# One transformer layer on one core: softmax reciprocals moved from GpSimd to VectorE, routing ahead of other deferred work, and a new order of the last rows

## The chip, the cores and the metric

The kernel runs on one core of one Trainium2 chip. The core has a matrix engine (TensorE, PE in the profile), VectorE (DVE), ScalarE (ACT), GpSimd (POOL) and queues that start DMA transfers; SyncE's queue is SP. Each engine runs its own instructions in order and waits on semaphores for the others. The metric is the device time in microseconds (us) of one execution, as the median of several.

## The reference

The layer is `x = x + LN(attention(LN(x)))`, then `x = x + LN(ffn(LN(x)))`, in fp32, with 1024 rows of 512 elements. `LN` subtracts the mean and divides by the root of the variance plus 1e-5, without weights.

- Attention: `q = x @ w_q` gives 32 heads of 128, `k` and `v` 8 heads of 128, each shared by 4 query heads. Scores are scaled by 1/sqrt(128), masked causally, and go through a softmax; the weighted values of all heads are multiplied by `w_o` (4096 x 512).
- FFN: `base = x @ base_W.T + base_b`. A router gives 15 logits; their softmax is taken, the 8 largest are kept, and each is added to one of 8 experts by `expert_map`. The low-rank part is `h = x @ A.T` (8 experts of rank 16), scaled by the weight of its expert, times `B`, times 2, and is added to `base`.

## The kernel before

**Blocks.** The rows are cut into eight tiles of 128 (t = 0 to 7), and the heads into eight groups g of four query heads and one key head. A block is a pair (g, t); a row pair u is tiles 2u and 2u + 1. Groups 0 to 5 run over all tiles in turn; then groups 6 and 7 are taken together for the row pairs 0, 3, 2, 1, so the rows end in the order 0, 1, 6, 7, 4, 5, 2, 3 (`blocks`, lines 86 to 90). In the code c, d, e, f are the rows 4, 5, 2 and 3 that end last (line 657).

**One block.** `scores` (line 385) is called four times for a block, for sub-tiles j of 32 rows by 4 heads, which makes 128 partitions. For each: PE forms the scores `s` in PSUM, n columns of them up to the diagonal; DVE adds the mask to the last 32 columns (line 406) and takes the negated row maximum `nmax` (line 408); ACT takes the exponential into `p` with the row sum `total` (line 413); POOL takes `rec = total ** -1` (line 415). `finish`, run after the exponential of the next sub-tile has been put out, scales `p` by `rec` on ACT (line 420) and transposes it in 32 x 32 squares on DVE (line 424) into `T`. After the fourth sub-tile, `to_keys` (line 436) copies `T` into `K` with 16 DMAs, on SyncE's queue for nearly all blocks. Two blocks later `weighted_values` (line 446) multiplies `K` by `v` on PE (`po`), and ACT copies the result to `attnT`.

**Buffers.** Scores have two PSUM tiles of 1024 columns; in rows 0 to 3 two sub-tiles share one, so an odd one begins when the even one's exponential is through. All other products (`pq`, `pk`, `pv`, `pl`, `pf`, `ptx`, `ptw`, `pa` to `pe`, `pO`) share three PSUM banks (`bank`, line 239).

**Output projection.** For groups 0 to 6, `project_o_pair` (line 492) multiplies two row tiles at once by `w_o` in seven products `pa` to `pe`, with four sums of `attnT` blocks on DVE (`sums`, lines 501 to 504) and combined weights that POOL prepares (`combine_o`, line 478). The last group has the plain `project_o` (line 463, `pO`). When its sum is complete, `ffn_norms` (line 551) normalises the row, adds x and normalises again to `h`.

**FFN of a row.** `ffn_router` (line 569) transposes `h` on PE and copies it to `hT` with ACT, then multiplies it by the router and low-rank weights (`pl`). `route` (line 590) is a chain of nine small DVE steps from `recr` to `hw`. `ffn_out` (line 619) adds up `pf` from four base products, transposes `hw` (`ptw`) and adds the low-rank product; then y is normalised, on POOL for the rows that end early and on DVE for e and f, added to `acc`, and stored.

**Order.** PE's instructions, and all that pass through `keep` (line 92), stand in program order; other instructions are placed by a scheduler that estimates when each can run. `defer` (line 367) puts pieces of the FFN into a list; each call of `scores` works off one or more from its head (line 416). In the main loop (lines 773 to 802) each block's PE pieces (projections of q, k and v for later blocks, output projections, FFN products) are woven into one list, and a quarter of it by columns follows each sub-tile's scores (`run_share`, line 720). The tail (lines 805 to 820) has an order written out by hand. `prepare_ffn` (line 201) has six DMA issues on POOL and the casts of `emap_f`.

Of the kernel before, what the change touches and what calls it, by code (L numbers as in the profile page):

```python
# [22 lines left out]
def kernel(  # L23
# [145 lines left out]
    make_identity(nc, ident)  # L169
    neg_half = const.tile([P, 1], F32, tag="neg_half", name="neg_half")  # L170
    nc.gpsimd.memset(neg_half, -0.5)
    neg_one = const.tile([P, 1], F32, tag="neg_one", name="neg_one")
    nc.gpsimd.memset(neg_one, -1.0)

    xnT = [big.tile([P, KC, QB], F32, tag=f"xnT{b}", name=f"xnT_{b}") for b in range(NQB)]

# [41 lines left out]
    def layernorm(dst, src, name, by=nc.vector):  # L218

        got = []  # L220

        def statistics():
            stats = small.tile([P, 6], F32, tag="stats", name=f"stats_{name}")
            order(nc.vector.bn_stats(stats, src))
            mv = small.tile([P, 2], F32, tag="mv", name=f"mv_{name}")
            order(nc.vector.bn_aggr(mv, stats))
            ve = small.tile([P, 1], F32, tag="ve", name=f"ve_{name}")
            order(nc.vector.tensor_scalar(ve, mv[:, 1:2], EPS, None, ALU.add))
            rstd = small.tile([P, 1], F32, tag="rstd", name=f"rstd_{name}")
            order(nc.gpsimd.tensor_tensor(rstd, ve, neg_half, ALU.pow))  # L230
            got.extend((mv, rstd))

        def norm():
            mv, rstd = got
            order(by.tensor_scalar(dst, src, mv[:, 0:1], rstd, ALU.subtract, ALU.mult))

        return statistics, norm

    def bank(name):
        return ps_m.tile([P, 512], F32, tag="pm", name=name)  # L240

    def bank_pv(name):
        return ps_m.tile([P, 512], F32, tag="po", name=name, bufs=1)
# [120 lines left out]
    score_tile = {}  # L364
    deferred = []

    def defer(*steps):

        if score_tile:
            deferred.extend(steps)  # L370
        else:
            for step in steps:
                step()
# [5 lines left out]
    def finish_scores():  # L379


        if "finish" in score_tile:
            score_tile.pop("finish")()

    def scores(g, t, j):

        n = t * P + (j + 1) * SQ
        full = (t + 1) * P
        name = f"{g}_{t}_{j}"

        if t < TPB and j % 2:
            s = score_tile.pop(0)[:, QB:]
        else:
            s = ps_s.tile([P, S], F32, tag="s", name=f"s_{name}")
            score_tile[0] = s
        for c0 in range(0, n, QB):
            w = min(QB, n - c0)
            matmul(
                s[:, c0 : c0 + w],
                qTs[g, t // 2][:, (t % 2) * NSUB + j, :, :].rearrange("p h q -> p (h q)"),  # L400
                kTs[g, c0 // QB][:, :w],
                start=True,
                stop=True,
            )
        pin = keep if blocks.index((g, t)) >= N2 + 2 else lambda ins: ins
        pin(nc.vector.tensor_tensor(s[:, n - SQ : n], s[:, n - SQ : n], smask, ALU.add))  # L406
        nmax = small.tile([P, 1], F32, tag="nmax", name=f"nmax_{name}")
        pin(nc.vector.tensor_reduce(nmax, s[:, :n], AX.X, ALU.max, negate=True))  # L408
        p = act.tile([P, S], F32, tag="p", name=f"p_{name}", bufs=3)
        if n < full:  # L410
            nc.gpsimd.memset(p[:, n:full], 0.0)  # L411
        total = small.tile([P, 1], F32, tag="total", name=f"total_{name}")
        nc.scalar.activation(p[:, :n], s[:, :n], AF.Exp, bias=nmax, accum_out=total)  # L413
        rec = small.tile([P, 1], F32, tag="rec", name=f"rec_{name}")
        nc.gpsimd.tensor_tensor(rec, total, neg_one, ALU.pow)  # L415
        work_off(1 + len(deferred) // 5)
        finish_scores()

        def finish():
            keep(nc.scalar.mul(p[:, :n], p[:, :n], rec))  # L420
            if j == 0:
                turned[g, t] = turn_view(turn_tile("T", g, t), t)
            pin(
                nc.vector.transpose(  # L424
                    turned[g, t][:, :, j, :, :].rearrange("p b k q -> p k b q"),
                    p[:, :full].rearrange("p (k b q) -> p k b q", b=R, q=SQ),
                )
            )
            if j == NSUB - 1:
                three = (nc.sync, nc.sync, nc.gpsimd)  # L430
                alone = 3 <= blocks.index((g, t)) < N - 1
                to_keys(g, t, by=three[:1] if alone else three)

        score_tile["finish"] = finish

    def to_keys(g, t, by=(nc.sync,)):

# [131 lines left out]
    def ffn_router(t):  # L569
# [5 lines left out]

        def products():
            hT = state["hT", t]
            pl = bank(f"pl_{t}")[:, : NR + ER]
            for c in range(KC):
                matmul(pl, hT[:, c, :], ra_sb[:, c, :], start=(c == 0), stop=(c == KC - 1))  # L580
            lg = small.tile([P, NR], F32, tag="lg", name=f"lg_{t}")
            order(nc.vector.tensor_tensor(lg, pl[:, :NR], rb_bc, ALU.add))
            nmax = small.tile([P, 1], F32, tag="nmax", name=f"nmaxr_{t}")
            order(nc.vector.tensor_reduce(nmax, lg, AX.X, ALU.max, negate=True))
            ex = small.tile([P, NR], F32, tag="ex", name=f"ex_{t}")
            total = small.tile([P, 1], F32, tag="total", name=f"totalr_{t}")
            nc.scalar.activation(ex, lg, AF.Exp, bias=nmax, accum_out=total)
            defer(lambda: route(pl, ex, total))

        def route(pl, ex, total):  # L590
            rec = small.tile([P, 1], F32, tag="rec", name=f"recr_{t}")
# [27 lines left out]
    def ffn_out(t):  # L619

        pf = []

        def base(c):
            if c == 0:
                pf.append(bank(f"pf_{t}"))
            matmul(pf[0], state["hT", t][:, c, :], weights["base", c], start=(c == 0), stop=False)

        def turn_hw():
            pt = bank(f"ptw_{t}")
            transpose(pt[:, :ER], state.pop(("hw", t)).rearrange("p e r -> p (e r)"), ident)  # L630
            hwT = state["hwT", t] = ffn.tile([ER, P], F32, tag="hwT", name=f"hwT_{t}")
            nc.scalar.copy(hwT, pt[:, :P])

        def finish():
            matmul(pf[0], state.pop(("hwT", t)), bt_sb, start=False, stop=True)
            y = ffn.tile([P, H], F32, tag="hy", name=f"y_{t}", bufs=3)
            order(nc.vector.tensor_tensor(y, pf[0], bias_bc, ALU.add))
            by = nc.vector if t in (e, f) else nc.gpsimd
            statistics, norm = layernorm(y, y, f"y{t}", by)

            def add_y():
                norm()
                order(by.tensor_tensor(acc[t], y, acc[t], ALU.add))
                state["done", t] = True

            defer(statistics, add_y)

        w = [(512, lambda c=c: base(c)) for c in range(KC)]
        return w[:2], [(P, turn_hw)], w[2:], [(512, finish)]
# [10 lines left out]
    def projections(i):  # L660
# [22 lines left out]
        else:  # L683
            n = i - N2
            for k, what in ((0, (G - 1, 0)), (2, (G - 2, 1)), (3, (G - 1, 1))):
                if n == k:
                    other += project_k(*what)
            for t in {0: (0,), 1: (1,), 2: (2, 3), 3: (4, 5), 4: (6, 7)}.get(n, ()):
                other += project_v(g // GV, t)
        return q, other  # L690

    def loads(i):
# [6 lines left out]
        if i < N2:  # L699
            if t == 3:  # L700
                load_k(g + 1)
            if t == 5 and g + 1 == G - 2:
                load_k(G - 1)
            if t == 6 and (g + 1) % GV == 0:
                for j in range(2):
                    load_v((g + 1) // GV, j)
            if t == 5:
                load_o(g + 1)
        elif i == N2 + 3:
            load_o(G - 1)  # L710
        elif i == N2 + 4:
            load_base("wk", (0, 1))
        elif i == N2 + 5:
            load_base("wv", (2, 3))

    def run(pieces):
# [53 lines left out]
    def attend(i):  # L770
        return weighted_values(*blocks[i])

    for i in range(N):
        loads(i)
        for t in complete(i, 2):
# [10 lines left out]
        for t in complete(i, 5):  # L786
            begins = ffn_router(t)

        rest = o + weave(o_pair, begins[1:] + other + pv)
        then = begins[:1] + q + ends[:-1] + rest[:4] + ends[-1:] + rest[4:]  # L790
        for n in range(NSUB):
            scores(*blocks[i], n)
# [2 lines left out]
            combine_o(0)  # L795
        if i == NT:
            prepare_ffn()
        for t in complete(i, 7, 8):
            ffn_store(t)

        if i >= NT and blocks[i - 2][1] == 0 and blocks[i - 2][0] < G - 1:
            combine_o(blocks[i - 2][0])


    finish_scores()
    score_tile.clear()
    work_off(len(deferred))
# [2 lines left out]
    (turn_d, products_d), (turn_e, products_e), (turn_f, products_f) = map(ffn_router, (d, e, f))  # L810
    out_c, out_d, out_e, out_f = map(ffn_out, (c, d, e, f))
    o_pair = project_o_pair(*pairs[N // 2 - 2])
    run([turn_d] + weave(o_pair, [products_d] + attend(N - 2)))
    run(out_c[0] + out_c[1] + out_c[2] + attend(N - 1) + out_c[3])
    run(project_o(*blocks[N - 2]) + out_d[0] + project_o(*blocks[N - 1]))
    run(out_d[1] + out_d[2] + out_d[3])
    run([turn_e] + out_e[0][:1] + [products_e] + out_e[0][1:] + out_e[2])
    run([turn_f] + out_f[0] + [products_f] + out_e[1] + out_e[3] + out_f[2] + out_f[1] + out_f[3])
    for t in (c, d, e, f):
        ffn_store(t)  # L820


# [39 lines left out]
```

## Time and profile before

The median of 3 runs is 1117.16 us (1116.51 to 1117.96).

| What | Value |
|---|---|
| profiled execution, its own time | 1116.45 us |
| span from the first to the last instruction | 1114.7 us |
| mean granted PE clock | 0.992 |
| PE busy | 1077.6 us (97%) |
| DVE busy | 631.1 us (57%) |
| ACT busy | 464.5 us (42%) |
| POOL busy | 264.5 us (24%), of it 141.6 in 256 reciprocals (553 ns each) |
| PE waits for `hw` at `ptw` | 7.7 us in 3 waits |
| PE waits for exponentials at `s` | 7.5 us in 10 waits |

Busy time is given by engine; an idle engine costs time only where the work that ends last waits for it. A row of the page's list of groups has the source line, the engine, the operation, output and inputs with their shapes, the count, then the busy time in us and the mean duration in ns, and the idle time before. A row of the timeline has the start, the duration, then the same names, and in brackets how long the engine stood idle and for what. An fp32 product of 512 columns shows as two instructions, each about 0.43 us apart.

### The profile page before, as it was taken

To read this page: it belongs to the slowest core of one execution; us is meant where nothing else is said; L and a number is where in the kernel's file an instruction comes from. 1 tells how busy PE (TensorE), PEld (TensorE's weight loads), DVE (VectorE), ACT (ScalarE), POOL (GpSimd) and SP (SyncE) were. 2 spreads that over 40 slices of the span, in tenths; PEclk is the share of its full clock that TensorE was granted. 3 is DMA by queue.
4 is the path that set the end of the run, shared out by engine and by line. 5 is a ranking of instruction groups with operands and counts; after the bars stand their busy time and mean duration, and the time that the engine had idled before them with its cause. 6 is when DMAs were issued, how large, how long until landed. Compare 5 with 4: busy or idle time off the path is not lost.

```text
span 1114.7 us, 12767 instructions
## 1 busy us (share of the span) xinstructions
PE 1077.6 (97%) x3836; PEld 708.0 (64%) x3836; DVE 631.1 (57%) x1267; ACT 464.5 (42%) x985; POOL 264.5 (24%) x562
## 2 busy tenths in 40 slices
PE   8899999999999999999999999999999999989894
PEld 7576666667676666666676666666776556556442
DVE  4465545664465546665465545665336665665744
ACT  2554524444344434544344434543335443433400
POOL 2621123111321113111221123111131212323421
PEclk9999999999999999999999999999999999999997
DMA  5135352555135432455125432456234464451310
GB/s 179 39 104 139 70 116 57 142 129 112 34 90 132 90 86 58 120 138 122 35 70 149 95 85 56 124 135 164 61 124 114 114 158 97 111 155 41 94 46 28
DMA packets 79060, 111.82 MB, mean 100 GB/s; under 512 B 18176, under 2 KB 50560, under 8 KB 78992
## 3 DMA queue, kind: packets, MB, share of 16 engines
q1 hardware_dynamic: 52976, 82.08, 31.7%
q10 hardware_dynamic: 25040, 27.27, 7.7%
q0 software_dynamic: 976, 1.65, 0.6%
q8 instruction: 31, 0.51, 0.2%
q14 instruction: 37, 0.30, 0.1%
HBM read 33.34 MB, written 2.10 MB: 32 GB/s over the span
## 4 chain that ended last, share of the span: by engine, by line
PE 78%; DVE 7%; SPq 4%; ACT 4%; POOL 3%; DMA 2%; issue 2%; ACTq 0%; POOLq 0%
PE po L100 19%; PE s L100 17%; PE pq L100 16%; PE pv L100 5%; PE pk L100 4%; PE pa L100 4%; SPq L106 4%; PE pe L100 4%; PE pb L100 2%; DVE T L424 2%; PE pd L100 2%; ACT p L413 2%; PE pc L100 2%; PE pf L100 2%; ACT p L420 2%
## 5 line engine op out<-in xcount | busy, mean ns | idle before, releaser
L413 ACT ACTIVATE p<-s,nmax 128x32 f32<-128x32 f32 (+31 forms) x256 | 179.3, 700 | 416.4 <-DVE nmax L408 402.2
L424 DVE STREAM_TRANSPOSE T<-p 128x128 f32<-128x128 f32 (+7 forms) x256 | 198.8, 777 | 232.3 <-ACT p L420 209.5
L415 POOL TENSOR_TENSOR rec<-total,neg_one 128x1 f32<-128x1 f32 x256 | 141.6, 553 | 627.1 <-ACT p L413 623.3
L100 PE MATMUL s<-kT,qT 128*128 128x512 f32 (+15 forms) x768 | 273.7, 465 | 7.5 <-ACT p L413 7.5
L100 PE MATMUL po<-K,v 128*128 128x512 f32 x576 | 276.4, 594 | 1.3 <-DMA K<-T 0.7
L100 PE MATMUL pq<-xnT,wq 128*128 128x256 f32 x1024 | 235.8, 380 | 0.0
L100 PEld LDWEIGHTS s<-kT,qT 128*128 128x128 f32 x768 | 145.5, 191 | 133.3 <-issue 109.0
L100 PEld LDWEIGHTS pq<-xnT,wq 128*128 128x128 f32 x1024 | 193.3, 190 | 38.1 <-issue 15.5
L420 ACT ACTIVATE p<-p,rec 128x32 f32<-128x32 f32 (+31 forms) x256 | 185.3, 724 | 6.7 <-POOL rec L415 6.5
L408 DVE TENSOR_REDUCE nmax<-s 128x1 f32<-128x32 f32 (+31 forms) x256 | 180.9, 707 | 7.9
L100 PEld LDWEIGHTS po<-K,v 128*128 128x128 f32 x576 | 107.6, 190 | 75.8 <-issue 65.9
L406 DVE TENSOR_TENSOR s<-s,smask 128x32 f32<-128x32 f32 x256 | 48.9, 191 | 132.9 <-PE s L100 132.3
L100 PE MATMUL pv<-wv,xnT 128*128 128x256 f32 x256 | 68.0, 381 | 0.7 <-ACT xnT L250 0.7
L336 ACT ACTIVATE qT<-pq 128x512 f32<-128x512 f32 x64 | 38.0, 593 | 70.5 <-PE pq L100 70.5
L411 POOL MEMSET p<- 128x96 f32 (+2 forms) x192 | 28.8, 151 | 160.5 <-DVE T L424 156.1
L100 PE MATMUL pk<-xnT,wk 128*128 128x512 f32 x128 | 64.5, 593 | 0.0
L100 PE MATMUL pa<-wo,attnT 128*128 128x256 f32 x224 | 62.0, 386 | 0.0
L452 ACT COPY attnT<-po 128x512 f32<-128x512 f32 x64 | 37.1, 580 | 51.0 <-PE po L100 50.4
L100 PEld LDWEIGHTS pv<-wv,xnT 128*128 128x128 f32 x256 | 48.1, 191 | 10.4 <-issue 2.7
L100 PEld LDWEIGHTS pa<-wo,attnT 128*128 128x128 f32 x224 | 41.4, 192 | 17.6 <-issue 13.8
L413 ACT ACTIVATION_READ_ACCUMULATOR p<-s,nmax 128x1 f32 x256 | 49.6, 194 | 0.0
L100 PE MATMUL pf<-wbase,hT 128*128 128x512 f32 x64 | 34.4, 662 | 3.8 <-DVE hw L609 3.1
(107 smaller groups left out, 771.8 us busy)
## 6 DMA issues: line engine op xcount, KB each, us to landing
K<-T SPq DMA_DIRECT2D x128, 128.0 KB, 2.4
K<-T SPq DMA_DIRECT2D x128, 112.0 KB, 2.3
wq<-in_w_q_dram ACTq DMA_DIRECT2D x27, 512.0 KB, 4.9
K<-T SPq DMA_DIRECT2D x128, 96.0 KB, 2.2
K<-T SPq DMA_DIRECT2D x128, 80.0 KB, 2.1
K<-T SPq DMA_DIRECT2D x123, 64.0 KB, 2.0
wo<-in_w_o_dram ACTq DMA_DIRECT2D x28, 256.0 KB, 3.8
K<-T SPq DMA_DIRECT2D x123, 48.0 KB, 1.9
```

Of the source, the lines that this page charges most:

```text
L100: keep(nc.tensor.matmul(*args, **kw))
L106: keep(by.dma_start(dst, src))
L336: nc.scalar.mul(qTs[g, u][:, :, j - 1 : j + 1, :].rearrange("p s h q -> p h s q"), pm[0].rearrange("p (h s q) -> p h s q", h=2, q=SQ), scale,)
L406: pin(nc.vector.tensor_tensor(s[:, n - SQ : n], s[:, n - SQ : n], smask, ALU.add))
L408: pin(nc.vector.tensor_reduce(nmax, s[:, :n], AX.X, ALU.max, negate=True))
L411: nc.gpsimd.memset(p[:, n:full], 0.0)
L413: nc.scalar.activation(p[:, :n], s[:, :n], AF.Exp, bias=nmax, accum_out=total)
L415: nc.gpsimd.tensor_tensor(rec, total, neg_one, ALU.pow)
L420: keep(nc.scalar.mul(p[:, :n], p[:, :n], rec))
L424: nc.vector.transpose(turned[g, t][:, :, j, :, :].rearrange("p b k q -> p k b q"), p[:, :full].rearrange("p (k b q) -> p k b q", b=R, q=SQ),)
L452: nc.scalar.copy(o, po)
```

## The change

- **Reciprocal.** `rec` becomes a DVE reciprocal. It and the scaling by ACT form a new step, `rescale`, which is run at the head of the next call of `scores`, ahead of its mask, so the scaling stands ahead of the next exponential. `finish` keeps the transpose and `to_keys`, and comes before the deferred work. Mask, maximum, exponential and scaling are in program order in every block.
- **Normalisation of y** for the rows other than e and f is done by ACT (with a shift computed on DVE) instead of POOL.
- **Routing** goes to the head of the deferred list.
- **Banks.** After the last scores, `pl` and the `pf` of rows e and f take halves of the score tiles.
- **PE order.** The value projection of row 7 for the last groups is moved two blocks back, the base weights that follow it in their buffer are loaded two blocks later, the router product of a block stands further back among its pieces, and the runs of the tail are in another order.
- **Stores** of finished rows are issued once the row is done instead of at a fixed block.

```diff
+            if by is nc.vector:
+                order(by.tensor_scalar(dst, src, mv[:, 0:1], rstd, ALU.subtract, ALU.mult))
+                return
+            shift = small.tile([P, 1], F32, tag="shift", name=f"shift_{name}")
+            order(nc.vector.tensor_scalar(shift, mv[:, 0:1], rstd, -1.0, ALU.mult, ALU.mult))
+            nc.scalar.activation(dst, src, AF.Identity, bias=shift, scale=rstd)
...
+    def bank_ffn(name):
+
+        if not score_tile:
+            if not spare:
+                both = ps_s.tile([P, S], F32, tag="s", name=f"s_{name}")
+                spare.extend((both[:, :512], both[:, 512:]))
+            return spare.pop(0)
+        return bank(name)
...
         if score_tile:
-            deferred.extend(steps)
+            deferred[:0] = steps if first else ()
+            deferred.extend(() if first else steps)
...
+    def rescale_scores():
+        if "rescale" in score_tile:
+            score_tile.pop("rescale")()
...
-        pin(nc.vector.tensor_tensor(s[:, n - SQ : n], s[:, n - SQ : n], smask, ALU.add))
+        rescale_scores()
+        keep(nc.vector.tensor_tensor(s[:, n - SQ : n], s[:, n - SQ : n], smask, ALU.add))
...
-        nc.scalar.activation(p[:, :n], s[:, :n], AF.Exp, bias=nmax, accum_out=total)
-        rec = small.tile([P, 1], F32, tag="rec", name=f"rec_{name}")
-        nc.gpsimd.tensor_tensor(rec, total, neg_one, ALU.pow)
+        keep(nc.scalar.activation(p[:, :n], s[:, :n], AF.Exp, bias=nmax, accum_out=total))
+        finish_scores()
         work_off(1 + len(deferred) // 5)
-        finish_scores()
+
+        def rescale():
+            rec = small.tile([P, 1], F32, tag="rec", name=f"rec_{name}")
+            keep(nc.vector.reciprocal(rec, total))
+            keep(nc.scalar.mul(p[:, :n], p[:, :n], rec))
 
         def finish():
-            keep(nc.scalar.mul(p[:, :n], p[:, :n], rec))
...
-            pl = bank(f"pl_{t}")[:, : NR + ER]
+            pl = bank_ffn(f"pl_{t}")[:, : NR + ER]
...
-            defer(lambda: route(pl, ex, total))
+            defer(lambda: route(pl, ex, total), first=True)
...
-                pf.append(bank(f"pf_{t}"))
+                pf.append(bank_ffn(f"pf_{t}") if t in (e, f) else bank(f"pf_{t}"))
...
-            for t in {0: (0,), 1: (1,), 2: (2, 3), 3: (4, 5), 4: (6, 7)}.get(n, ()):
+            for t in {0: (0,), 1: (1,), 2: (2, 3), 3: (4, 5), 4: (6,)}.get(n, ()):
                 other += project_v(g // GV, t)
+            if n == 6:
+                q = project_v(g // GV, 7)
...
-        elif i == N2 + 5:
+        elif i == N2 + 7:
             load_base("wv", (2, 3))
...
-        rest = o + weave(o_pair, begins[1:] + other + pv)
+        rest = o + weave(o_pair, other + pv[:2] + begins[1:] + pv[2:])
...
-        for t in complete(i, 7, 8):
+        ready += complete(i, 7, 8)
+        for t in [t for t in ready if ("done", t) in state]:
+            ready.remove(t)
             ffn_store(t)
...
-    run([turn_d] + weave(o_pair, [products_d] + attend(N - 2)))
-    run(out_c[0] + out_c[1] + out_c[2] + attend(N - 1) + out_c[3])
-    run(project_o(*blocks[N - 2]) + out_d[0] + project_o(*blocks[N - 1]))
-    run(out_d[1] + out_d[2] + out_d[3])
-    run([turn_e] + out_e[0][:1] + [products_e] + out_e[0][1:] + out_e[2])
-    run([turn_f] + out_f[0] + [products_f] + out_e[1] + out_e[3] + out_f[2] + out_f[1] + out_f[3])
+    run([turn_d] + weave(o_pair[:8], attend(N - 2)) + [products_d] + o_pair[8:])
+    run(out_c[0] + out_c[1] + out_c[2] + attend(N - 1))
+    run(project_o(*blocks[N - 2]) + out_c[3] + project_o(*blocks[N - 1]))
+    run(out_d[0] + out_d[1] + out_d[2] + [turn_e] + out_d[3] + [products_e])
+    run(out_e[0] + out_e[2][:1] + [turn_f] + out_e[2][1:] + [products_f])
+    run(out_f[0] + out_e[1] + out_f[2][:1] + out_e[3] + out_f[2][1:] + out_f[1] + out_f[3])
```

More of the change, by code (lines that the diff above doesn't have):

```diff
@@ L171 @@
     nc.gpsimd.memset(neg_half, -0.5)
-    neg_one = const.tile([P, 1], F32, tag="neg_one", name="neg_one")
-    nc.gpsimd.memset(neg_one, -1.0)
     xnT = [big.tile([P, KC, QB], F32, tag=f"xnT{b}", name=f"xnT_{b}") for b in range(NQB)]
@@ L234, in norm @@
             mv, rstd = got
-            order(by.tensor_scalar(dst, src, mv[:, 0:1], rstd, ALU.subtract, ALU.mult))
+            if by is nc.vector:
[4 more added lines that the diff above has]
+            nc.scalar.activation(dst, src, AF.Identity, bias=shift, scale=rstd)
         return statistics, norm
@@ L240, in bank @@
         return ps_m.tile([P, 512], F32, tag="pm", name=name)
+    spare = []
+    def bank_ffn(name):
[5 more added lines that the diff above has]
+        return bank(name)
     def bank_pv(name):
@@ L365, with defer @@
     deferred = []
-    def defer(*steps):
+    def defer(*steps, first=False):
         if score_tile:
-            deferred.extend(steps)
+            deferred[:0] = steps if first else ()
+            deferred.extend(() if first else steps)
         else:
@@ L405, in scores @@
         pin = keep if blocks.index((g, t)) >= N2 + 2 else lambda ins: ins
-        pin(nc.vector.tensor_tensor(s[:, n - SQ : n], s[:, n - SQ : n], smask, ALU.add))
+        rescale_scores()
+        keep(nc.vector.tensor_tensor(s[:, n - SQ : n], s[:, n - SQ : n], smask, ALU.add))
         nmax = small.tile([P, 1], F32, tag="nmax", name=f"nmax_{name}")
-        pin(nc.vector.tensor_reduce(nmax, s[:, :n], AX.X, ALU.max, negate=True))
+        keep(nc.vector.tensor_reduce(nmax, s[:, :n], AX.X, ALU.max, negate=True))
         p = act.tile([P, S], F32, tag="p", name=f"p_{name}", bufs=3)
@@ L432, in finish @@
                 to_keys(g, t, by=three[:1] if alone else three)
-        score_tile["finish"] = finish
+        score_tile["rescale"], score_tile["finish"] = rescale, finish
     def to_keys(g, t, by=(nc.sync,)):
@@ L638, in finish @@
             by = nc.vector if t in (e, f) else nc.gpsimd
-            statistics, norm = layernorm(y, y, f"y{t}", by)
+            statistics, norm = layernorm(y, y, f"y{t}", nc.vector if t in (e, f) else nc.scalar)
             def add_y():
@@ L771, in attend @@
         return weighted_values(*blocks[i])
+    ready = []
     for i in range(N):
@@ L802 @@
             combine_o(blocks[i - 2][0])
+    rescale_scores()
     finish_scores()
@@ L812 @@
     o_pair = project_o_pair(*pairs[N // 2 - 2])
-    run([turn_d] + weave(o_pair, [products_d] + attend(N - 2)))
-    run(out_c[0] + out_c[1] + out_c[2] + attend(N - 1) + out_c[3])
-    run(project_o(*blocks[N - 2]) + out_d[0] + project_o(*blocks[N - 1]))
-    run(out_d[1] + out_d[2] + out_d[3])
-    run([turn_e] + out_e[0][:1] + [products_e] + out_e[0][1:] + out_e[2])
-    run([turn_f] + out_f[0] + [products_f] + out_e[1] + out_e[3] + out_f[2] + out_f[1] + out_f[3])
-    for t in (c, d, e, f):
+    run([turn_d] + weave(o_pair[:8], attend(N - 2)) + [products_d] + o_pair[8:])
[4 more added lines that the diff above has]
+    run(out_f[0] + out_e[1] + out_f[2][:1] + out_e[3] + out_f[2][1:] + out_f[1] + out_f[3])
+    for t in (*ready, c, d, e, f):
         ffn_store(t)
```

## The prediction

> **What bounds the kernel now.** I read the page's totals and slices first, then TensorE's (PE's) waits, then PE's busy time by stretch, and last the rows around its longest gaps.
>
> ```profile
> span 1114.7 us, 12767 instructions
> PE 1077.6 (97%) x3836; PEld 708.0 (64%) x3836; DVE 631.1 (57%) x1267; ACT 464.5 (42%) x985; POOL 264.5 (24%) x562
> ...
> PEclk9999999999999999999999999999999999999997
> ...
> L415 POOL TENSOR_TENSOR rec<-total,neg_one 128x1 f32<-128x1 f32 x256 | 141.6, 553 | 627.1 <-ACT p L413 623.3
> ```
>
> PE is busy 97% of the span, so the 141.6 us that POOL spends on reciprocals are no measure of a gain: only PE's 37 us of idle time, and its slow clock in the last slice, can be won. No matrix product is removed. Where PE waits:
>
> ```profile
> PE ptw L103 <- DVE hw L609: 7.7, 3, 3.4
> PE s L100 <- ACT p L413: 7.5, 10, 1.5
> PE pf L100 <- DVE hw L609: 3.1, 1, 3.1
> ```
>
> (us in total, times, longest). The largest cause is the routing result `hw`, 10.8 us; then scores waiting for an exponential to free their bank. By stretch (length, PE busy, ..., granted clock, DMA share, GB/s):
>
> ```profile
> 500.00:700.00 200.00, 199.31 (x726) 134.84 (x725) 108.27 (x212) 86.11 (x191) 44.01 (x98) 1.00 0.37 87
> ...
> 900.00:1000.00 100.00, 94.54 (x320) 56.55 (x319) 63.56 (x138) 39.91 (x81) 24.87 (x46) 0.98 0.51 126
> ...
> 1080.00:1095.00 15.00, 11.21 (x36) 5.68 (x35) 8.85 (x28) 1.68 (x5) 5.53 (x6) 0.92 0.05 17
> 1095.00:1114.70 19.70, 8.76 (x18) 3.83 (x16) 8.10 (x23) 0.93 (x4) 1.11 (x2) 0.67 0.07 27
> ```
>
> The middle loses 0.7 us in 200; the losses sit at the start, around 985, and after 1040. The rows there:
>
> ```profile
> 985.32 1.49 DVE L504 TENSOR_TENSOR sums<-attnT,sums 128x256 f32<-128x256 f32 x1
> ...
> 989.54 0.30 PE L103 MATMUL ptw<-ident,hw 128*128 128x128 f32 x1 [3.37 <-DVE hw L609]
> 989.68 2.97 PE L100 MATMUL pf<-wbase,hT 128*128 128x512 f32 x4
> ...
> 1052.81 1.25 PE L100 MATMUL pl<-ra_sb,hT 128*128 128x143 f32 x8 [1.97 <-ACT hT L250]
> ...
> 1091.87 2.91 PE L100 MATMUL pf<-wbase,hT 128*128 128x512 f32 x4 [3.11 <-DVE hw L609]
> ...
> 1099.59 0.45 PE L103 MATMUL ptw<-ident,hw 128*128 128x128 f32 x1 [3.10 <-DVE hw L609]
> ```
>
> At 989.54 `hw` of row 6 comes last, because its chain (about 2.0 us from `recr` to `hw`) stood behind four `sums` additions (the last took 1.49 us), a mask and a row maximum. At 1091.87 and 1099.59 PE waits for the routing of the last two rows with nothing else to do. After these gaps four 512-wide products take 2.9 to 3.0 us; the same four took 1.88 at 984.29.
>
> **The change, part by part.** Sums are against the profiled execution, 1116.45 us (span 1114.7 and 1.75 around it); the median is 0.7 us above it, which I add at the end.
>
> *Reciprocal.* POOL loses 256 x 0.553 us, off the path but for the start: there POOL runs four subtractions of 1.26 us from 40.87 to 46.17 ahead of `rec`, and two score products wait 1.30 and 1.03 us behind it. VectorE (DVE) gains 256 x 0.156 us (row "RECIPROCAL recr", 0.156) = 40 us, some 43 with gaps, at 57% busy. I followed the queues forward from the second of these waits: the score comes at about 51.65 instead of 53.25, **gain 1.6**, between 0 and 2.5. In the middle the scaling (`mul`) goes ahead of the next exponential instead of behind it, but now follows a DVE reciprocal, about 0.2 us with its hand-over. Queued behind that waiting reciprocal are the next mask and maximum; the exponential waits for them and, in rows 0 to 3, an odd sub-tile's score waits for its partner's exponential. The cover is PE's pace: 3.5 us per sub-tile in rows 0 to 3 and 3.0 to 4.7 in the others, against a DVE-ScalarE round of 3.0 us for row 2. So the reciprocal costs nothing as long as PE's own work covers it. What is not covered is a side effect of pinned masks: in even rows the four `sums` (0.40 + 3 x 0.42), which wait for `attnT`, now stand ahead of reciprocal, mask and maximum. In row 2 that delays the exponential by 1.1 to 1.4 us, against a slack of 0.14 us in even groups and less in odd ones: about 0.7 us in each of three odd groups, 0.4 twice and 0.15 three times for row 0, **loss 3.4** with the other groups' small remainders. Bounds: a gain of 1, since three gaps of 0.7 at row 3 may close, and a loss of 12, if every group's even rows stall by 0.5 to 1.
>
> *FFN constants.* POOL's six DMA issues stand at 147.5 to 151.3 and DVE waits 6.4 us for the last, `emap_i`, ahead of `emap_f`. Without reciprocals POOL reaches them at about 139, so they land before the mask that now stands behind `emap_f`: **gain 0.7** (the 0.72 us stall at 157.47). Were they not earlier, that mask and its score would be late by 6.5 us.
>
> *Value projection of row 7, two blocks later.* At 866.24 PE waits 1.43 us for `attnT`, itself queued behind a `mul`; 1.72 us of projection now lie ahead, and `attnT` precedes that `mul`: **gain 1.4**. The weights it shares a buffer with are loaded two blocks later, two issues of 0.35 to 0.5 us on ScalarE's queue, first needed a block later, so free. One block on, a new wait of about 0.3.
>
> *Routing first, score products later.* At 906 `hw` comes 1.2 us earlier, but `hT` of row 1 is queued behind a scaling and an exponential, about 2.3 us; with 0.9 us at 916.76 gone, net **0.3**. At 985 the routing passes the sums: its gap of 3.37 us closes and the four products regain 2.97 - 1.88 = 1.1 us, **gain 4.4**. SyncE's queue: the store of a finished row no longer holds the transfers behind it (at 1054.98 a store waited for POOL's addition, ended 1054.95, while the last `T` had been done since 1053.03).
>
> *y on ScalarE.* Nearest row for the normalisation: `mul` at 512 elements, 0.712 us, against 2.08 on POOL, and a shift of 0.15 on DVE. It frees POOL but stands in ScalarE's queue ahead of `hT` copies.
>
> *The tail.* From 1025.4 PE's gaps before are 0.67 + 1.46 + 1.97 + 0.86 + 0.19 + 0.67 + 3.11 + 3.10 + 0.41 + 0.41 = 12.85 us. From 1091.87 to 1107.69 PE has 12 instructions of 0.43, 8 of 0.13 and two transposes of 0.29, 6.8 us at full clock; the stretch less its gaps is 11.9, so 5.1 are lost to the clock: 18.0 in all. After, walking each queue with these durations: scores of row 3 wait 1.4; `po` of (7,2) waits for its transposed block, `T` done at 1041.2, 16 issues of 0.635 on SyncE, 2 to land, 1053.4, while PE is through with the pieces ahead of it at 1050.3, a gap of 3.1; `ptw` of row 5 waits 0.9 for a `y`; `pl` of rows 2 and 3 wait 1.6 and 2.05 for `hT` behind ScalarE's `y`; the shared bank costs 0.5; small rest 0.6. Sum 10.1, last addition at 1103.6 instead of 1111.48: **gain 7.9**. The routing of the last rows is covered by the products moved behind it. Lower bound 3 (each wait for `hT` a microsecond longer, clock lost twice), upper 11 (the gaps of `po` and `hT` away).
>
> [...] The gap of 3.1 us at `po` is the place where the change could lose what it gains. Rows: gaps of 3.37 and 3.11 us were followed by half the pace, 1.97 was not. [...] By the rows it is at the edge: 1.1 us as at 989.54, up to 2. I take 0.8, half of 1.5.
>
> Sum: 1.6 - 3.4 + 0.7 + 1.4 - 0.3 + 0.3 + 4.4 + 7.9 - 0.8 = 11.8. Profiled 1104.7, as a median **1105.4 us**.
>
> **Rivals.** (a) *The tail's gaps move more than they vanish*: `po` of (7,2) and three `hT` waits grow, the clock drops there instead. For it: SyncE's issue takes 10.2 us whatever comes first, and ScalarE's queue is longer. Against: the changed order puts three `o` products ahead of the wait. Tail gain 3 instead of 7.1: about 1109.5. (b) *The middle costs nothing* and the tail closes further, because `sums` ahead of a mask find `attnT` ready: 3.4 + 2 more, about 1100. Against it: the copy to `attnT` that the sums wait for lands, in even rows, about when the mask is ready to run. (c) *The score chain becomes the bound*, slower: the reciprocal at the head of DVE's queue adds 0.22 us per sub-tile in rows 2 to 5, 128 sub-tiles, 28 us in full. It decides from 0.12 us per sub-tile (15.2 us of other gains / 128). For it: row 2's round is 3.0 us and will be 3.2 with the sums. Against: the 0.7 us of idle time in 200 us shows that PE, not the chain, sets this pace. In full 1117.2 - 15.2 + 28 = 1130. (d) *No effect*: queues re-form so that gains at 985 and the tail are given back, 1117.
>
> **How the numbers follow.** Likeliest 0.47, (a) 0.22, (b) 0.18, (c) 0.08, (d) 0.05. The likeliest alone spans 1101 to 1108. The range of 8 in 10 reaches to both (a) and (b) with their bounds, 1097 to 1113, and leaves out (c) and (d) and tails of the rest. A measurement here tells 0.2%, 2.2 us, from no change. Faster: 0.47 + 0.22 + 0.18 and a part of (d), 0.88; same 0.04; slower 0.08.
>
> **What would show it.** No `rec` on POOL; `hw` of row 6 before the sums near 985 and no gap over 1 us at its `ptw`; granted clock of the last stretch above 0.9; no gap over 2.5 us after the last score except at `po` of (7,2); gaps at `s` in row 2 of groups 1, 3 and 5, with `sums` ahead of the mask. The prediction is wrong if score waits in the middle sum to over 10 us, or if the last stretches stay at half clock.

## The result and the profile after

The changed kernel takes 1104.81 us (median of 4 runs, 1102.96 to 1106.09) against 1116.84 us before (4 runs): a ratio of 0.989, 95% interval 0.9873 to 0.9907. The forecast was 1105.4 us. The profiled execution took 1105.28 us with a span of 1103.5.

The page's totals of the changed kernel:

```profile
PE 1074.5 (97%) x3836; PEld 704.5 (64%) x3836; DVE 654.0 (59%) x1529; ACT 491.2 (45%) x991; POOL 113.8 (10%) x299
```

POOL lost 150 us of work and PE only 3 of busy time; PE is busy for 97% of the span, as before. PE's waits after (us in total, times, longest):

```profile
PE s L100 <- ACT p L433: 8.6, 17, 1.2
PE po L100 <- DMA K<-T: 2.6, 1, 2.6
PE s_pf L100 <- ACT hT L264: 1.5, 1, 1.5
...
PE ptw L103 <- DVE y L659: 0.9, 1, 0.9
```

No wait for `hw` is left, where there were 11.7 us: the 10.8 of the prediction's rows and 0.9 at one `pb`. Scores wait longer for exponentials than before, 8.6 us in 17 places instead of 7.5 in 10. Busy time by stretch (length, PE busy, ..., granted clock, DMA share, GB/s):

```profile
500.00:700.00 200.00, 198.26 (x722) 134.04 (x722) 111.32 (x257) 89.58 (x188) 15.79 (x46) 1.00 0.36 86
...
900.00:1000.00 100.00, 100.00 (x342) 60.03 (x341) 65.72 (x169) 44.00 (x86) 11.28 (x26) 1.00 0.47 119
...
1080.00:1095.00 15.00, 11.84 (x42) 6.08 (x42) 10.90 (x37) 3.27 (x10) 4.14 (x4) 1.00 0.10 36
```

From 900 to 1000 PE has no idle time left (94.54 of 100 before), the middle is worse than before (198.26 of 200 instead of 199.31), and the stretch from 1080 to 1095 runs at full clock (0.92 before). Around row 6's routing:

```profile
985.38 0.29 DVE L631 TENSOR_TENSOR hw<-pl,w 128x128 f32<-128x128 f32 x1
985.69 0.43 DVE L523 TENSOR_TENSOR sums<-attnT 128x256 f32<-128x256 f32 x1
985.79 1.88 PE L100 MATMUL pf<-wbase,hT 128*128 128x512 f32 x4
...
987.51 0.27 PE L103 MATMUL ptw<-ident,hw 128*128 128x128 f32 x1
```

`hw` is ready ahead of the sums (at 985.67) and 1.8 us before PE takes it.

To see where the time went, I compare the start of the first score product of every sub-tile in two traces, counted from the first score of the kernel. That first score comes at 24.84 us before and at 26.31 after, but also between 24.7 and 27.6 in the kernels below, with and without any one part of the change (24.75 in the last one, which holds all of it). It goes with the pace of PE's first products. Eight `pv` products near 8 us take 2.0 us in the four traces whose first score comes at 24.7 to 24.8 (in the kernel before at a granted clock of 1.00 from 8 to 12), and 3.4 to 3.7 in the four where it comes at 26.2 to 26.5, the changed kernel among them (3.65, at a granted clock of 0.50). In the four where it comes at 27.5 to 27.6 they take 3.8, and the eight transposes behind them 1.9 instead of 1.0 to 1.2; in two of these, the runs `sums_later` and `k_split`, the granted clock reads 1.00 from 8 to 12, so what slows them there is not shown. Since the time of the first score goes with no part of the change, the first 25 us are not counted to it. Lengths in us:

| stretch of work | before | after | gain | predicted |
|---|---|---|---|---|
| first score to row 4 of group 0 | 37.63 | 36.78 | 0.85 | 1.6 |
| to the last score of group 5 | 694.14 | 699.18 | -5.04 | -3.4 + 0.7 |
| from there over rows 0, 1, 6, 7, 4, 5 of groups 6 and 7 | 226.75 | 222.60 | 4.15 | 1.4 - 0.3 + 0.3 |
| rows 2 and 3 to the last score | 64.19 | 57.58 | 6.61 | 4.4 and a part of the tail |
| last score to last addition | 63.93 | 57.86 | 6.07 | rest of 7.1 in the tail |
| sum | 1086.64 | 1074.00 | 12.64 | 11.8 |

The sum fits the forecast better than its terms do. The experiments were made for the terms.

### The profile page after: what moved, and what is told of

It reads as the page before. It is cut to its first block, busy times and chain, and to the rows that moved or that the text cites. A ratio compares the mean times of both kernels' runs of the same rounds, so it can differ in the third digit from the quotient of the medians.

```text
span 1103.5 us, 12827 instructions
## 1 busy us (share of the span) xinstructions
PE 1074.5 (97%) x3836; PEld 704.5 (64%) x3836; DVE 654.0 (59%) x1529; ACT 491.2 (45%) x991; POOL 113.8 (10%) x299
## 3 DMA queue, kind: packets, MB, share of 16 engines
q0 software_dynamic: 976, 1.65, 0.6%
## 4 chain that ended last, share of the span: by engine, by line
PE 82%; DVE 7%; ACT 5%; DMA 2%; issue 1%; SPq 1%; POOL 1%; ACTq 0%; POOLq 0%; DVEq 0%
PE po L100 20%; PE s L100 18%; PE pq L100 16%; PE pk L100 4%; PE pv L100 4%; PE pe L100 4%; PE pa L100 3%; ACT p L433 2%; PE pO L100 2%; PE pc L100 2%; PE pb L100 2%; PE pd L100 2%; DVE T L446 2%; PE pf L100 2%; DVE nmax L428 2%; ACT p L440 2%
## 5 line engine op out<-in xcount | busy, mean ns | idle before, releaser
L440 ACT ACTIVATE p<-p,rec 128x32 f32<-128x32 f32 (+31 forms) x256 | 187.9, 734 | 179.3 <-DVE rec L439 121.0
L439 DVE RECIPROCAL rec<-total 128x1 f32<-128x1 f32 x256 | 39.8, 155 | 55.1 <-ACT p L433 53.2
L523 DVE TENSOR_TENSOR sums<-attnT 128x256 f32<-128x256 f32 x28 | 11.9, 425 | 56.8 <-ACT attnT L474 56.7
```

Source lines behind the costliest of these rows:

```text
L439: keep(nc.vector.reciprocal(rec, total))
L523: nc.vector.tensor_tensor(s1, a21, a22, ALU.add)
```

## The experiments

Each ratio compares a run with the kernel before on the same chip. That kernel took 1115.91 to 1117.15 us on these chips, so a distance from the changed kernel, which is one of medians, is good to about 1 us. A stretch of the traces is not exact either: to the last score of group 5, the routing and the tail, each alone, gain 0.7 and 0.9 us, at one place, row 1 of group 1, which they do not touch. Parts of the change were tried alone or left out, one cost was tripled, one suspected order was undone, and two gaps were attacked.

### The order of the sums

```diff
+        def add_up():
+            nc.vector.tensor_tensor(s1, a21, a22, ALU.add)
...
-        return (
+        return [(1, add_up)] + (
             product("a", 0, a11, b11)
...
+        first, o_pair = o_pair[:1], o_pair[1:]
-        then = begins[:1] + q + ends[:-1] + rest[:4] + ends[-1:] + rest[4:]
+        then = first + begins[:1] + q + ends[:-1] + rest[:4] + ends[-1:] + rest[4:]
```

> The changed kernel with the four sums put out behind the block's first scores instead of ahead of them. Theory: in the even blocks the sums, which wait for attnT, stand ahead of reciprocal, mask and maximum, and this alone costs the middle its 1.0 us per odd group in row 0, 0.6 per even group, 0.8 in row 2, some 6.9 us in all; without it 1098 to 1101 us. Rival: the reciprocal on VectorE and the scaling ahead of the exponential cost these stalls; then they stay, 1104 to 1106 us.

Measured: 1100.31 us, ratio 0.9854 (0.9841 to 0.9868), 4.5 us below the changed kernel. In the kernel before, the mask of group 5, row 2 stands ahead of the sums:

```profile
670.74 0.20 DVE L406 TENSOR_TENSOR s<-s,smask 128x32 f32<-128x32 f32 x1 [1.76 <-PE s L100]
670.87 0.42 DVE L501 TENSOR_TENSOR sums<-attnT 128x256 f32<-128x256 f32 x1
...
673.12 0.70 PE L100 MATMUL s<-kT,qT 128*128 128x320 f32 x2
```

The same place in the changed kernel:

```profile
676.29 0.43 DVE L523 TENSOR_TENSOR sums<-attnT 128x256 f32<-128x256 f32 x1 [3.40 <-ACT attnT L474]
...
677.43 0.42 DVE L526 TENSOR_TENSOR sums<-attnT,sums 128x256 f32<-128x256 f32 x1
...
677.76 0.15 DVE L439 RECIPROCAL rec<-total 128x1 f32<-128x1 f32 x1
677.84 0.18 DVE L426 TENSOR_TENSOR s<-s,smask 128x32 f32<-128x32 f32 x1
...
679.25 0.81 PE L100 MATMUL s<-kT,qT 128*128 128x320 f32 x2 [0.54 <-ACT p L433]
```

and with the sums behind the first scores:

```profile
672.80 0.51 ACT L440 ACTIVATE p<-p,rec 128x256 f32<-128x256 f32 x1
672.81 0.20 DVE L426 TENSOR_TENSOR s<-s,smask 128x32 f32<-128x32 f32 x1 [2.40 <-PE s L100]
672.94 0.43 DVE L525 TENSOR_TENSOR sums<-attnT 128x256 f32<-128x256 f32 x1
...
675.19 0.70 PE L100 MATMUL s<-kT,qT 128*128 128x320 f32 x2
```

In the changed kernel the reciprocal, although its input had been ready for over 4 us (exponential at 672.99, accumulator at 673.36), stands behind four sums that wait for `attnT`; mask, scaling and exponential follow it, and PE waits. With the sums moved, the scaling and the mask run at once and the score has no wait. The stretch to the last score of group 5 is 693.83 us long instead of 699.18, 0.3 shorter than before the change. So the middle's loss is the place of the sums, and the reciprocal on DVE costs the middle nothing that the traces can tell once they are out of its way. That the pinned mask, and not the reciprocal ahead of it, let the sums come first is argued from the edit; the two were not tried apart. Of the 6.9 us of stalls that I had added up, 5.35 were won by the traces; the others were given back later in the row anyway.

### The reciprocal alone, left out, and tripled

The first part alone on the kernel before (`rescale` and its pins, as in the diff above), and the changed kernel with POOL's power and the late scaling again:

> The kernel before with the first part of the change alone: reciprocal on VectorE, scaling ahead of the next exponential, these pinned in order. Theory: gains some 1 us at the start, loses 5 in the middle, 1119 to 1121 us, slower than before. Rival: freeing POOL is a large part of the gain, 1110 us or less.

> The changed kernel with the reciprocal on POOL and the scaling where they were before. Theory: the gain comes from the order of routing and tail; without the reciprocal's loss in the middle 1101 to 1103 us. Rival: the tail needs POOL free, 1106 to 1110 us.

Measured: alone 1115.12 us, ratio 0.9991 (0.998 to 1.0002), a difference that the runs do not tell from none; left out 1106.53 us, 0.991 (0.9895 to 0.9925), 1.7 us above the changed kernel, with intervals that overlap. Both theories miss: alone it was not slower, and without it the kernel was not faster; 1106.53 lies in the range of the second rival, that the tail needs POOL free. By stretch, against before: alone +0.85, -5.05, +4.24, +0.67, +2.82; the change without it +0.02, +0.29, +1.34, +4.84, +3.77. The loss in the middle is all this part's, as expected; I had not seen that the same part wins 4.2 us in the third stretch (rows 0, 1, 6, 7, 4, 5) and 2.8 in the tail. Two places, 2.9 of the 4.2, are in the traces: the scaling, now ahead of the exponential, no longer stands ahead of the `attnT` copy at the start of row 6 (step of 1.70 us where PE waited 1.43), and row 0's `hw` is ready before PE wants it (1.22 us). The value projection's move was meant for the first of these too; either of the two edits closes it, so their gains do not add. Of the 2.8 in the tail, 1.7 is only PE's pace: behind the same wait of 3.1 us for `hw`, `pf` and `pl` take 1.96 and 1.15 us instead of the 2.91 and 1.91 before, where the granted clock is 0.50 from 1092.73 to 1096.14. In the change without this part, `po` of block (7,2) waits 3.46 us instead of 2.64, which speaks for the rival in part.

```diff
             keep(nc.vector.reciprocal(rec, total))
+            for _ in range(2):
+                keep(nc.vector.reciprocal(rec, rec))
```

> The changed kernel with each reciprocal followed by two more of the same kind on the same word (1/(1/(1/x)) is the same value up to rounding), 0.32 to 0.4 us more per sub-tile on VectorE ahead of the mask. Theory: PE covers it except where the trace shows a score waiting for an exponential (17 places): 1.0 to 1.5 times 0.35 x 17, 6 to 9 us, 1110 to 1114 us. Rival: the chain of VectorE and ScalarE sets the pace of rows 2 to 5, then 0.35 x 128 = 45 us or more, 1150 us.

Measured: 1114.59 us, ratio 0.9978 (0.9969 to 0.9987), 9.8 us above the changed kernel (8.6 counted from the first score). Waits of scores for exponentials go from 8.6 to 13.2 us, still in 17 places, those for `attnT` from 1.1 to 3.4. Twice 0.16 us in each of 256 sub-tiles is over 80 us of work on the chain, of which about a tenth is seen. The chain is not the bound; it counts in the places where PE already waited.

### Routing and tail, each alone

The kernel before with `first=True` for the routing and the stores issued once a row is done:

> The kernel before with the routing put at the head of the deferred list, and stores issued once a row is done, nothing else. Theory: the gap of 3.37 us at 989 closes and four products regain 1.1 us, 4.4 in all, and the routing ahead of other work gains 0 to 1 at 1040: 1111 to 1113 us. Rival: the order of the sums, not of the list, sets hw of row 6, so the gap stays: 1116 to 1118 us.

Measured: 1112.00 us, ratio 0.9962 (0.9947 to 0.9976). The step at the first score after row 6's `hw` is 4.43 us, as worked out (3.37 + 1.1). The kernel before with the new tail order and its banks:

> The kernel before with the new order of the tail and its banks alone. Theory: the gaps of 3.11 and 3.10 us and the half clock behind them go, less the new waits for hT: 5 to 7 us, 1110 to 1112 us. Rival: the tail needs the reciprocal and y off POOL, since POOL's y holds the row norms: 2 us or less, 1115 to 1117 us.

Measured: 1113.72 us, ratio 0.9977 (0.9969 to 0.9985): 3.0 us, between the two. In the trace the tail gives 3.27 us, and PE waits 3.0 us for `h` at `ptx_h`, which the changed kernel does not. The next run shows what that wait is. `po` of (7,2) waits 3.5 us there as well.

### y on POOL again

```diff
-            if by is nc.vector:
+            if True:
...
-            statistics, norm = layernorm(y, y, f"y{t}", nc.vector if t in (e, f) else nc.scalar)
+            statistics, norm = layernorm(y, y, f"y{t}", by)
```

> The changed kernel with the normalisation of y back on POOL. Theory: ScalarE's y of 0.81 us stands ahead of hT at 1080 and 1086, where PE waits 0.98 and 1.53 us; without it 1 to 1.5 us less, 1103.3 to 1104 us. Rival: POOL's 2.08 us hold the next row's rstd or its addition, 1106 us or more.

Measured: 1108.06 us, ratio 0.9921 (0.9906 to 0.9936), 3.3 us above the changed kernel: the rival. POOL, DVE and PE around it:

```profile
1079.85 2.08 POOL L234 TENSOR_SCALAR y<-y,mv_y,rstd_y 128x512 f32<-128x512 f32 x1
...
1082.49 1.48 DVE L234 TENSOR_SCALAR acc<-acc,mv_a,rstd_a 128x512 f32<-128x512 f32 x1 [3.24 <-POOL rstd_a L228]
...
1087.09 1.12 PE L103 MATMUL ptx_h<-ident,h 128*128 128x128 f32 x4 [3.00 <-DVE h L234]
```

The waits for `hT` behind ScalarE's y do go, as I held, but POOL's 2.08 us hold the next row's `rstd_a`, DVE waits 3.24 us for it, and PE 3.0 for `h`. Of the 3.3 us, the traces give 1.9 in the last stretch. Another 0.7 is a wait that the edit does not touch: a score in row 1 of group 1, behind the cast of the expert map, waits 1.45 us instead of 0.71, because the map landed later. The same wait for `h` took part of the tail's gain in the run with the tail alone. In the changed kernel ScalarE needs 0.81 us for y:

```profile
1086.03 0.81 ACT L238 ACTIVATE y<-y,shift_y,rstd_y 128x512 f32<-128x512 f32 x1 [0.88 <-DVE shift_y L237]
...
1087.37 1.25 PE L100 MATMUL s_pf<-ra_sb,hT 128*128 128x143 f32 x8 [1.53 <-ACT hT L264]
```

### The gap at block (7,2)

```diff
-                alone = 3 <= blocks.index((g, t)) < N - 1
+                alone = 3 <= blocks.index((g, t)) < N - 2
```

> The changed kernel with the 16 transfers of block (7,2) on SyncE and POOL instead of on SyncE alone. Theory: PE's gap of 2.64 us at 1048 closes, and with it the half clock behind it (pa in 1.91 instead of 1.03 us), 3 to 4 us in all, 1101 to 1102 us. Rival: PE comes to the next wait earlier and stands there (hT, attnT or a row norm), 1103.5 to 1105 us.

Measured: 1105.83 us, ratio 0.9902 (0.9889 to 0.9916), no gain. In the changed kernel PE waits for the last of 16 issues, and the products behind run at nearly half pace (`pa` in 1.91 us, against 1.03 at 1044.71):

```profile
1048.38 1.33 PE L100 MATMUL po<-K,v 128*128 128x512 f32 x2 [2.64 <-DMA K<-T]
...
1049.50 1.91 PE L100 MATMUL pa<-wo,attnT 128*128 128x256 f32 x4
```

With five transfers on POOL this gap is gone and another of 2.73 us stands at the last score:

```profile
1039.44 2.52 POOL L106 DMA_DIRECT2D K<-T  x5 [0.66 <-PE po L100]
...
1042.58 0.55 DVE L234 TENSOR_SCALAR h<-acc,mv_h,rstd_h 128x512 f32<-128x512 f32 x1 [2.59 <-POOL rstd_h L228]
...
1046.54 1.13 PE L100 MATMUL s<-kT,qT 128*128 128x512 f32 x2 [2.73 <-ACT p L433]
```

The five issues take POOL 2.5 us; row 5's `rstd_h` stands behind them, DVE waits for it ahead of a mask and a maximum, and the exponential that frees the score bank is late. By the traces the last stretch is 3.0 us shorter than in the changed kernel and the one before it 2.0 longer; 0.8 more is again the score behind the map, where no edit was made. The expectation had not named what stands in POOL's queue behind the issues. In the last run the five issues follow one sub-tile later, behind `rstd_h`; it also holds the moved sums and an earlier issue of the FFN constants, and these two alone are the run ahead of it.

```diff
+                if (g, t) == blocks[N - 2] and n % 3 == 2:
+                    late.append((dst[ts(b, SQ), h], src[ts(h, SQ), b]))
...
         work_off(1 + len(deferred) // 5)
+        if (g, t) == blocks[N - 1] and j == 0:
+            load_late()
...
-        if i == NT:
+        if i == NT - 2:
             prepare_ffn()
+        if i == NT:
+            prepare_map()
```

> The changed kernel with the sums behind the first scores and the FFN constants' transfers issued two blocks ahead of their cast. Theory: VectorE no longer waits 2.5 us for the map ahead of a mask, the score's wait of 0.7 us in row 1 of group 1 goes: 1099 to 1100 us. Rival: what the wait cost is regained before the row's end anyway (the step of 0.9 at one score is followed by one of 1.0 the other way): 1100 to 1101 us.

> The changed kernel with three edits together: the sums behind the first scores, the FFN constants' transfers issued two blocks ahead of their cast, and five of the 16 transfers of block (7,2) on POOL, but put out one sub-tile later, so that they stand behind the row norm's rstd_h. Theory: 4.5 us from the sums, 0.7 from the constants, and now 3 from the gap at po of (7,2) and the half clock behind it, since nothing waits behind POOL's issues: 1096 to 1098 us. Rival: PE's wait comes back at the next score or attnT whatever the order on POOL: 1099 to 1101 us.

Measured: sums and constants 1100.64 us, ratio 0.986 (0.9843 to 0.9877), the same as with the sums alone: the rival, no cost of the constants' wait can be told in the end. With the late transfers 1094.73 us, ratio 0.9812 (0.9797 to 0.9827), the fastest of all, 10.1 us below the changed kernel (8.7 by the two ratios, 8.8 counted from the first score).

```profile
1030.53 0.55 POOL L231 TENSOR_TENSOR rstd_h<-ve_h,neg_half 128x1 f32<-128x1 f32 x1 [0.96 <-DVE rec L444]
...
1031.43 2.51 POOL L106 DMA_DIRECT2D K<-T  x5 [0.35 <-PE s L100]
...
1039.68 1.13 PE L100 MATMUL po<-K,v 128*128 128x512 f32 x2 [1.31 <-ACT attnT L489]
1040.64 1.03 PE L100 MATMUL pa<-wo,attnT 128*128 128x256 f32 x4
```

The same five issues now hold nobody; a wait of 1.31 us for `attnT` is left, and `pa` is back at 1.03 us. Against the run without the late transfers the last stretch is 2.99 us shorter by the traces; of the 5.9 us between the two medians the other part, some 2.8, is the early first score (24.75 against 27.59). That is PE's pace at the start, and is not counted to the edit.

## Why the prediction was right, and where its steps were not

- **Start, 1.6.** Right in kind: `rec` no longer waits behind POOL's subtractions. It was 0.85 by the trace: 0.49 + 0.93, less 0.56 lost at row 1.
- **Middle, -3.4.** The mechanism, sums pinned ahead of reciprocal, mask and maximum, was right, and the run with the sums moved shows it. The size was off: row 2 of the odd groups cost 0.7 to 0.8 as said, but row 0 cost 1.1 in odd groups and 0.6 in two even ones, where the sum had 0.15 and 0.4. There the last scaling of row 7, 1.15 us, also stands ahead of row 0's first exponential. The three gaps at row 3 or 4, which the bound let close, gave back only 0.4 to 0.6 each.
- **FFN constants, 0.7.** Failed. POOL reached the issues at 142.3 us, not 139, and the step assumed that earlier issues land before they are needed; `emap_i` landed 7.5 us after its issue and DVE still waited 2.5. The wait of 0.72 that was to be won is, by the row, one of `po` for a transfer of `K`, not for the map, and it is not in the trace of the tail alone, so there was nothing sure to win.
- **Value projection, 1.4 - 0.3.** The 1.43 us wait went (net 1.6 by the steps), but the order of scaling closes it alone.
- **Row 1's `hT`, net 0.3.** Failed: no PE wait is left between 900 and 1000, the gain was 2.4: 1.2 at row 0's `hw`, the rest at the next two scores. I had put the router product where `hT` would be 2.3 us late; the new weave puts it at 917.79, and `hT` is done at 910.76.
- **Routing at 985, 4.4.** Right: 4.6, and 4.43 alone.
- **Tail, 7.9 less 0.8 for the clock.** Right in sum and mostly in place: scores of row 3 0.70 for 1.4, `po` 2.64 for 3.1, `ptw` 0.93 for 0.9, `hT` 0.98 and 1.53 for 1.6 and 2.05, the shared bank 0.50 for 0.5. The clock term was right in its place, 0.9 us in `pa`, but its size was my estimate, half of the 1.5 us taken from the rows: in the traces the slow products went with where a gap fell, not with its length (last section). What the working did not say is that the tail needs y off POOL: I gave that edit no price, and it is worth 1.9 us by the traces, 3.3 by the medians.

The signs that the prediction named hold: score waits sum to 4.7 us from 100 to 900, not over 10, and after the last score only `po` of (7,2) has a gap over 2.5 us. The granted clock is 1.00 from 1080 to 1095; in the last 8.5 us it is 0.61, against the sign, but PE has two instructions there.

Of the rivals, the score chain as the bound fell with the tripled reciprocal, the middle at no cost with its loss of 5 us, and no effect with the result. That the tail's gaps move rather than vanish is true of single repairs (`k_split`), not of the change as a whole. The two terms that gained more than was said, in rows 6 and 4, made up for the start and the middle, which gained less or lost more (2.75 us against 3.1), so that the total came out by luck closer than its parts.

## What to carry to other kernels

When an edit pins instructions that a scheduler had placed freely, look at what unpinned work now falls ahead of the pins: here four additions that waited for a late copy cost the middle 5 us, and the moved reciprocal itself cost it nothing that could be told. A small transfer issue or normalisation on an idle-looking engine is priced by what is queued behind it, such as a one-word `rstd`; the same five issues cost 2.7 us of a PE wait, or nothing, by one sub-tile's place. Parts of a change that close the same wait do not add, so try each part alone before its gain is booked, and compare stretches as well as medians, since PE's pace can move either: here by 1.7 us in the tail with the first part alone, and by 2.8 at the start between the last two runs.

## What the runs showed of the hardware

- A PE gap of 2.64 us was followed by nearly half pace (`pa` 1.91 us instead of 1.03), yet one of 2.73 in `k_split` was not (granted clock 1.00 from 1045.24 to 1048.65). The granted clock that the profiler recorded in the traces of the kernel before (from 7.30 us on) and the changed one (from 1.22) is 1.00 or 0.50, and the stretches between its changes are 3.41 us long or whole multiples of it, but for the last, in which the recording ends. The steps around the gap in the changed kernel (1045.74 to 1048.38), then in `k_split` (1043.81 to 1046.54; length, PE busy, ..., granted clock, DMA share, GB/s):

```profile
1045.70:1049.11 3.41, 0.77 (x3) 0.49 (x3) 3.27 (x13) 2.05 (x6) 0.62 (x1) 1.00 0.22 54
1049.11:1052.53 3.42, 3.42 (x7) 2.03 (x6) 1.94 (x4) 0.45 (x1) 1.59 (x4) 0.50 0.20 44
```

```profile
1041.83:1045.24 3.41, 1.97 (x11) 1.14 (x9) 2.35 (x7) 1.02 (x3) 0.77 (x3) 1.00 0.44 112
1045.24:1048.65 3.41, 2.11 (x7) 1.11 (x8) 2.72 (x11) 1.52 (x4) 0.55 (x1) 1.00 0.16 38
```

The first gap lies in one step, and PE is busy for 0.77 us of it; the second is split between two, with 1.97 and 2.11. With PE's busy time as the profile models it, the kernel before has four full-clock steps of 3.41 us that were followed by half clock, from 986.92, 1089.31, 1096.14 and 1106.38 on, with PE busy for 0.79, 0.86, 0.35 and 1.13 us. The changed kernel has three, from 4.63, 1045.70 and 1093.48 on, with 1.43, 0.77 and 1.65. Of the full-clock steps that were not, the least busy has 1.95 us (before, from 1044.94). So in these two traces a step with PE busy for 1.65 us or less of 3.41 was followed by half clock and one with 1.95 or more was not; what lies between is not shown. The gap of 2.64 us left a step with 0.77 us of PE's work, the one of 2.73 none below 1.97.

- ScalarE's scale with a shift, 128 x 512, took 0.81 us, against 0.71 for its plain scaling of the same size, which the forecast had used.
- A DVE product of 120 elements took 1.27 us instead of 0.28 at 1087.06, just as POOL's addition of 1.27 us ran at 1086.92. Before the change the same was seen at 1053.80 (1.29 us). Whether the one took longer because of the other was not tried.
